# Counting 22 of 157 edge groups with matrix products instead of 24, and fetching 18 tiles of rows one row at a time from SyncE

## The chip, the core and the metric

The kernel runs on one core of a Trainium2 chip. Five engines work side by side, each through its own list of instructions in order: TensorE (PE; its weight loads are shown apart as PEld), VectorE (DVE), ScalarE (ACT), GpSimd (POOL) and SyncE (SP, which only issues transfers). They wait for each other by semaphores. The metric is the device time of one execution in microseconds (us).

## The reference

One layer of a graph network over 12500 nodes with 256 features and 200000 edges, sorted by their target `dst`. The sum over the edges is the part that this change touches.

```python
h = jnp.maximum(_layernorm(x, axis=-1), 0.0)
agg = jax.ops.segment_sum(h[src], dst, num_segments=N)
z = (1.0 + eps_gin) * h + agg
t = jnp.dot(z, W1) + b1
t = jax.nn.relu(_batchnorm(t, g1, bt1))
conv_out = jnp.dot(t, W2) + b2
out = jax.nn.relu(_batchnorm(conv_out + h, g2, bt2))
return x + out
```

## The kernel before

The edges are cut into 1563 tiles of 128 edges, and ten tiles make a group (`GT` = 10): 157 groups, the last one with three tiles. A group's edges all end in a narrow stretch of nodes, since the edges are sorted. `h_tab` in device memory holds for each node the 2 KB row of h, split into two parts that add up to full precision.

Most groups are **gathered groups**. For each of the ten tiles POOL issues one indirect transfer (`gather`, L665), which fetches 128 rows of `h_tab` by `src` into a place called `gt`; there are three such places (`RING` = 3), and the gather of a group waits until the group three before it has been read. VectorE builds ten one-hot matrices of `dst` (`edges`, L716), and TensorE multiplies the ten tiles of rows by them and adds them up in `ps` (`sums`, L748).

The other 24 groups are **counted groups**, in two sets of 12 (`SETS`, `JOINT`). They fetch no rows by index. The whole table `h_tab` is streamed past them instead, in 98 blocks of 128 nodes, through a ring of ten places (`stream`, loaded by SyncE at L963). For each counted group and each eight blocks there is one **unit**: VectorE marks which edge has its source in which of the eight blocks (`marks`, `mk`, L991), TensorE multiplies the marks by one-hots of the low seven bits of `src` (`fill`, L1008: ten products of 96 columns into `pm`), ScalarE copies the counts out of `pm` (L1012), TensorE multiplies the counts by the eight blocks (`weigh`, L1024: eight products of 512 columns), and VectorE adds the result to the group's accumulator (`collect`, L1041). A set of 12 groups takes 13 x 12 units, so there are 312 units in all. The low one-hots of a set lie in **homes**: three in a tile `away` (`AWAY` = 3), three in the still unused tile of the weights `w2s`, and twelve in `spread`.

Whichever way a group was summed, its result is then placed at its nodes: `hold` copies it (L809 to L811), `put` multiplies it by a one-hot (L834), `add` adds it into a chunk `zc` of 512 nodes (L851). A finished chunk is multiplied by W1 in four slices (`slice_of`, L861), each of which is written to `t_tab` by SyncE (L879).

The program has four stages. The lead stage (34 steps, one group each) computes h from x and sums the first 34 groups from x itself. The **middle stage** has one step for each remaining gathered group of the line except the last five. In a step the code issues one gather (four steps ahead), one sum, the placing of one or two groups, one or two slices, and as many units as `plan` has given this step: `plan` walks through the steps with two budgets (TensorE columns by a `rate`, VectorE cycles by `BUSY`), and the lowest rate is taken at which all units end in time. The works of a step are interleaved: unit, sum, placing, unit, placing or slice, and so on. A short stage then finishes the last groups, and the last stage applies the two normalisations and W2. The order of each engine's list is that of the code (`manual_schedule`).

SyncE's list in the middle stage holds the loads of `stream` (each waits until TensorE has read the block that lay there), the stores to `t_tab` (each waits for ScalarE's copy `ts`) and the loads of `zc`.

Of the kernel before, what the change touches and what calls it, by code (L numbers as in the profile page):

```python
# [9 lines left out]
F32 = mybir.dt.float32  # L10
F32R = mybir.dt.float32r
F8 = mybir.dt.float8e4
I32 = mybir.dt.int32
# [5 lines left out]
P = 128  # L19
# [5 lines left out]
LEAD = 34  # L25
# [6 lines left out]
SETS = 2  # L32
JOINT = 12
WIN = 12
# [3 lines left out]
BUSY = 12500  # L38
AWAY = 3
EASE = 3  # L40
# [9 lines left out]
def kernel(  # L50
# [328 lines left out]
    def fast():  # L379
# [24 lines left out]
        with ExitStack() as fs:  # L404
# [14 lines left out]
            with ExitStack() as es:  # L419
# [223 lines left out]

                groups = [(t0, min(GT, NTILE - t0)) for t0 in range(0, NTILE, GT)]
                gathered = {i: early[i] for i in range(EARLY)}
                landing = [tc.alloc_semaphore(f"whole{k}") for k in range(AHEAD + 1 + RING)]
# [6 lines left out]
                def gather(i):  # L653
# [7 lines left out]
                    else:  # L661
                        ga = ((0, GT, singles[k - EARLY]),)
                    for t in reversed(range(t0, t0 + n)):
                        rows = left if t == full_tiles else P
# [4 lines left out]
                        if i < NG - 2:  # L669
                            tc.no_tile_sem_insts.add(fetch.ins.name)  # L670
                            tc.add_to_no_dep_group(f"rows{i}", fetch.ins)
                            fetch.then_inc(inside if t > t0 else landing[place_of(i)], 16)
                    if i < NG - 2:
# [59 lines left out]
                def sums(i, among=()):  # L733
# [7 lines left out]
                    for k, j in enumerate(order):  # L741
# [4 lines left out]
                        if i >= LEAD:  # L746
                            lhsT, rhs, to = lhsT.bitcast(F32R), rhs.bitcast(F32R), ps.rearrange("p k d -> p (k d)")
                        reader = nc.tensor.matmul(to, lhsT=lhsT, rhs=rhs, start=(j == order[0]), stop=(j == order[-1]))  # L748
                        if waited:
                            behind(i, reader)  # L750
                            waited = False
# [341 lines left out]
                for i in range(LEAD):  # L1093
# [48 lines left out]

                    for n in range(max(JOINT * (i - LEAD + 4) // 4, 0), JOINT * (i - LEAD + 5) // 4):
                        low_digits(n)
                    sums(i, (puts, slice_ups))
# [29 lines left out]
                for s in range(LEAD, LAST):  # L1175
# [46 lines left out]
                    for k in range(1, max(len(counting), len(others) - 1)):  # L1222
                        works += counting[k : k + 1] + others[k + 1 : k + 2]
                    for work in works:
                        work()
                    while whole < NCH and all(k in done for k in touching[whole]):
                        queue += [(whole, f) for f in range(HC)]
                        whole += 1
# [605 lines left out]
```

## Time and profile before

| | |
|---|---|
| median of 3 runs | 2436.89 us (2431.2 to 2457.89) |
| the profiled execution | 2432.64 us, its span 2430.7 us |
| TensorE busy | 1808.9 us, 74% |
| VectorE busy | 1445.2 us, 59% |
| ScalarE busy | 826.6 us, 34% |
| GpSimd busy | 1332.5 us, 55% |
| mean granted TensorE clock | 0.879 |
| transfers | 513.28 MB, mean 211 GB/s |

Busy time is the union of an engine's instructions. Waiting, and the instructions that only issue transfers or set registers, do not count, so SyncE has no busy time; its transfers' issue appears as "SPq". The granted clock is the share of the full TensorE clock in that stretch. A line such as "POOL gt L665 <- PE ps L748" reads: the gather of line 665 stood idle until the sum of line 748 had finished.

### The profile page before, as it was taken

Reading aid. Unit: us, or ns where it says so; the run is one execution under the profiler, and the core shown is the slowest. Engines: PE = TensorE matmul, PEld = TensorE weight load, DVE = VectorE, ACT = ScalarE, POOL = GpSimd, SP = SyncE. Lnnn points to the kernel's source line nnn. Section 1 sums busy time; section 2 is a strip of 40 time slices with the busy share of each in tenths; the row PEclk is TensorE's granted clock in tenths of the full one; section 3 lists DMA queues with packets and bytes.
Section 4 is the critical chain, followed back from the end, with each engine's and each line's share of the span. In section 5 each row is a group of like instructions: output and inputs, shape, how many; then the busy total and the mean of one; then the engine's idle time right before and its main releaser. Section 6 shows DMA issues by size and latency. Waiting matters only on the chain. (4 is left out here: it accounts for less than half of the span.)

```text
span 2430.7 us, 25628 instructions
## 1 busy us (share of the span) xinstructions
PE 1808.9 (74%) x8988; PEld 1277.0 (53%) x8988; DVE 1445.2 (59%) x2244; ACT 826.6 (34%) x1608; POOL 1332.5 (55%) x1372
## 2 busy tenths in 40 slices
PE   1566666637787788888786788788787877658997
PEld 1444444525565566556554556566565655425445
DVE  4565666636466565565556655555555655544897
ACT  1675656613322222222221222222222222112555
POOL 7666666653565555556545565555555545442550
PEclk9876887868998999899987899999898988689999
DMA  5667677656676766666666676676776756466888
GB/s 165 206 221 237 205 244 222 196 154 198 209 217 201 209 197 209 195 213 203 214 179 190 202 239 205 194 213 201 215 212 198 220 180 219 126 172 218 307 306 335
DMA packets 195410, 513.28 MB, mean 211 GB/s; under 512 B 30358, under 2 KB 45626, under 8 KB 195272
## 3 DMA queue, kind: packets, MB, share of 16 engines
q0 software_dynamic: 94928, 302.21, 42.5%
q1 hardware_dynamic: 98960, 208.29, 25.1%
q8 instruction: 73, 1.20, 0.2%
q10 hardware_dynamic: 1384, 1.06, 0.2%
q14 instruction: 65, 0.53, 0.1%
HBM read 434.64 MB, written 76.80 MB: 210 GB/s over the span
## 5 line engine op out<-in xcount | busy, mean ns | idle before, releaser
L665 POOL DMA_INDIRECT gt<-h_tab,srcT x983 | 930.2, 946 | 786.2 <-PE ps L748 453.4
L1024 PE MATMUL pz<-stream,counts 128*120 128x512 f32 (+1 forms) x2352 | 702.3, 445 | 26.5 <-issue 14.2
L1012 ACT CAST counts<-pm 128x480 fp32r<-128x480 f32 (+1 forms) x600 | 308.2, 556 | 843.9 <-PE pm L1008 387.0
L1024 PEld LDWEIGHTS pz<-stream,counts 128*120 128x120 f32 (+1 forms) x2352 | 453.7, 204 | 136.1 <-issue 17.3
L991 DVE SCALAR_TENSOR_TENSOR mk<-col,dstT 128x960 fp8e4<-128x960 f32 (+5 forms) x328 | 340.8, 1043 | 0.0
L1041 DVE TENSOR_TENSOR gta<-pz,gta 120x512 f32<-120x512 f32 x192 | 132.3, 689 | 325.4 <-PE pz L1024 198.2
L716 DVE TENSOR_TENSOR oh<-col,dstT 128x1280 fp32r<-128x1280 f32 (+1 forms) x131 | 194.2, 1483 | 150.3 <-remote 87.0
L748 PE MATMUL ps<-gt,oh 128*128 128x512 f32 x970 | 259.7, 417 | 0.0
L861 PE MATMUL ph<-zc,w1s 128*128 128x512 f32 (+1 forms) x392 | 207.0, 657 | 49.7 <-issue 19.1
L748 PEld LDWEIGHTS ps<-gt,oh 128*128 128x128 f32 x970 | 199.8, 207 | 49.5 <-issue 1.0
L1008 PE MATMUL pm<-mk,spread 128*128 128x96 fp8e4 (+1 forms) x1560 | 100.9, 210 | 115.8 <-issue 49.8
L1008 PEld LDWEIGHTS <-spread 128*128 128x128 fp8e4 x1560 | 79.8, 101 | 170.4 <-issue 109.9
L878 ACT COPY ts<-ph 128x512 f32<-128x512 f32 x96 | 56.0, 584 | 331.5 <-issue 176.4
L1041 DVE TENSOR_TENSOR gtb<-pz,gtb 120x512 f32<-120x512 f32 x96 | 66.1, 689 | 152.5 <-PE pz L1024 94.5
L665 POOL DMA_INDIRECT stream<-in_x_dram,srcT x130 | 124.3, 956 | 57.4 <-issue 28.8
L851 DVE TENSOR_TENSOR zc<-pz,zc 128x512 f32<-128x512 f32 (+15 forms) x227 | 110.4, 513 | 72.1 <-PE pz L834 38.0
L861 PEld LDWEIGHTS ph<-zc,w1s 128*128 128x128 f32 x392 | 81.4, 214 | 124.8 <-issue 80.6
L872 DVE BATCH_NORM_STATS2 st<-ph 128x6 f32<-128x512 f32 x96 | 66.8, 696 | 132.1 <-PE ph L861 63.3
L834 PE MATMUL pz<-at,zh 128*128 128x256 f32 (+2 forms) x484 | 100.0, 318 | 56.2 <-issue 16.9
L834 PEld LDWEIGHTS pz<-at,zh 128*128 128x128 f32 (+1 forms) x484 | 79.4, 206 | 89.1 <-issue 39.7
L665 POOL DMA_INDIRECT gta<-in_x_dram,srcT x96 | 92.7, 966 | 50.4 <-issue 17.3
L1008 PE MATMUL pm<-mk,away 128*128 128x96 fp8e4 (+1 forms) x780 | 52.8, 215 | 74.2 <-DVE mk L991 33.3
(247 smaller groups left out, 2271.6 us busy)
## 6 DMA issues: line engine op xcount, KB each, us to landing
stream<-h_tab SPq DMA_DIRECT2D x201, 256.0 KB
h_tab<-gt SPq DMA_DIRECT2D x24, 1024.0 KB
t_tab<-ts SPq DMA_DIRECT2D x96, 256.0 KB
gt<-h_tab,srcT POOLq DMA_INDIRECT x983
gt<-in_x_dram SPq DMA_DIRECT2D x24, 512.0 KB
h_cols<-gt SPq DMA_DIRECT2D x24, 512.0 KB
zc<-h_cols SPq DMA_DIRECT2D x24, 512.0 KB
yT<-h_cols SPq DMA_DIRECT2D x24, 512.0 KB
```

The lines of the kernel that those rows point to most:

```text
L665: fetch = nc.gpsimd.indirect_dma_start(out=slot(ga, t - t0)[:rows], out_offset=None, in_=x if i < LEAD else h_tab, in_offset=bass.Indirect ...
L716: nc.vector.tensor_tensor(oh.bitcast(F32R) if i >= LEAD else oh, col[:, :P].unsqueeze(1).to_broadcast([P, n, P]), dstT[:, t0 : t0 + n].uns ...
L748: reader = nc.tensor.matmul(to, lhsT=lhsT, rhs=rhs, start=(j == order[0]), stop=(j == order[-1]))
L834: nc.tensor.matmul(pz[:, d, :n], lhsT=zs[:rows, k, d * P : (d + 1) * P].bitcast(F32R), rhs=at[:rows, :n].bitcast(F32R), start=(k == 0), st ...
L851: nc.vector.tensor_add(side, pz[:, :, a - lo : b - lo], side)
L861: nc.tensor.matmul(ph[:, :n], lhsT=w1s[:, d, f * P : (f + 1) * P], rhs=zc[c][:, d, :n], start=(d == 0), stop=(d == DC - 1),)
L872: nc.vector.bn_stats(st1[:, f, c, :], ph[:, :n])
L991: nc.vector.scalar_tensor_tensor(mk[:, :, done * WIN : done * WIN + w], col[:, :w].unsqueeze(1).to_broadcast([P, GT, w]), float(a0 * WIN), ...
L1008: nc.tensor.matmul(pm[:, k, :], lhsT=digits[z][j][:, t0 + k, :], rhs=marked[n][:, t0 + k, :w], start=True, stop=True,)
L1012: nc.scalar.copy(counts[n][:, :nb, :].bitcast(F32R).rearrange("p a (t d) -> p t a d", d=WIN)[:, t0 : t0 + m], pm.rearrange("p t (a d) -> p ...
L1024: nc.tensor.matmul(products[n][:ROWS], lhsT=counts[n][:rows, k, :].bitcast(F32R), rhs=ring[(b0 + k) % len(ring)][:rows].bitcast(F32R), sta ...
L1041: nc.vector.tensor_add(acc[j][:ROWS], got, acc[j][:ROWS])
```

## The change

**Two sets of 11 counted groups** (`JOINT` = 11). The line of gathered groups grows by two, from 133 to 135, and the middle stage from 94 to 96 steps. A set takes 13 x 11 units, so 286 are left of 312. The planner's lowest rate becomes 24400 (26500 before); its units end in step 126 (123 before). Of the steps, before and now, 6 and 25 have two units, 40 and 41 have three, 41 and 24 have four; three steps have another number.

**Homes.** `away` holds one home, not three, and `spread` eleven, not twelve, which makes room for two places of 128 x 512 numbers, called `apart`. The moments at which the second set's one-hots are written follow from the homes that come free, as before. Of the first set's one-hots seven are written in the three steps before the last of the lead stage and four in the last one (three in each step before).

**18 tiles row by row.** Every fifth step from step 42 to 127 the gathered group loses the first of its ten tiles: POOL issues nine indirect transfers for it. SyncE fetches that tile instead, over the five steps that end two steps before the sum: 28 rows in each of the first four, 16 in the fifth. At a step's first part SyncE reads 28 row numbers from a tile in on-chip memory into its registers (the tile `vrows`, whose 18 rows are loaded with the numbers at the start of the fast path). For each row it computes an address and issues one transfer of 2 KB. The rows are spread over the parts of the step, behind each part's own transfers. TensorE waits, ahead of the last of the ten products of that sum, for the semaphore of the tile's 128 rows.

SyncE's list around a boundary of two such steps, now (L1015 is the load of a `stream` block, L669 the reading of the row numbers, L679 the address and the row):

```order
L679 DMA apart<-h_tab 1x512
L1015 DMA stream<-h_tab 128x512
L669 TENSOR_LOAD vrows
L679 ISA
L679 DMA apart<-h_tab 1x512
L679 ISA
L679 DMA apart<-h_tab 1x512
```

The same list in the middle stage before (L963 is the load of a `stream` block, L879 the store of a slice, L705 the load of a chunk):

```order
L963 DMA stream<-h_tab 128x512 x2
L879 DMA t_tab<-ts 128x512
L963 DMA stream<-h_tab 128x512 x2
L879 DMA t_tab<-ts 128x512
L963 DMA stream<-h_tab 128x512 x3
L705 DMA zc<-h_cols 128x1024
L963 DMA stream<-h_tab 128x512 x7
```

Every load of a block and every store now has several pairs of address and row in front of it on the same queue.

ScalarE's list shows how many units a step has, since each unit has two copies of counts and each step begins with one L809. A stretch early in the middle stage, before (L1012 copies counts, L878 a slice):

```order
L809 CAST zh<-ps 128x256
L1012 CAST counts<-pm 128x5x8x12 x4
L878 COPY ts<-ph 128x512
L1012 CAST counts<-pm 128x5x8x12 x2
L809 CAST zh<-ps 128x256
L1012 CAST counts<-pm 128x5x8x12 x8
L809 CAST zh<-ps 128x256
```

And a stretch at about the same place now (the same copies, at lines 861, 1064 and 930):

```order
L861 CAST zh<-ps 128x256
L1064 CAST counts<-pm 128x5x8x12 x4
L930 COPY ts<-ph 128x512
L861 CAST zh<-ps 128x256
L1064 CAST counts<-pm 128x5x8x12 x8
L861 CAST zh<-ps 128x256
L1064 CAST counts<-pm 128x5x8x12 x8
L861 CAST zh<-ps 128x256
L1064 CAST counts<-pm 128x5x8x12 x6
```

Steps of two units with one slice have come in beside those of three and four. TensorE's list at a sum of a group that has lost a tile, before and now (the first row is a unit's `weigh`, the second the sum, then the placing):

```order
L1024 MATMUL pz_4265<-stream,counts 120x512 x8
L748 MATMUL ps<-gt,oh 128x512 x10
L834 MATMUL pz_4288<-at,zh 128x256 x4
L1008 LDWEIGHTS w2s
L1008 MATMUL pm<-mk,w2s 128x96
```

```order
L1076 MATMUL pz_6740<-stream,counts 120x512 x8
L795 MATMUL ps<-gt,oh 128x512 x9
L795 MATMUL ps<-apart,oh 128x512
L886 MATMUL pz_6829<-at,zh 128x256 x4
L1060 LDWEIGHTS away
```

Nine products read the gathered tiles, and the tenth reads the place that SyncE has filled. The diff:

```diff
-JOINT = 12
+JOINT = 11
...
-AWAY = 3
+AWAY = 1
+GAP = 5
+ASK = 28
...
                 groups = [(t0, min(GT, NTILE - t0)) for t0 in range(0, NTILE, GT)]
+                alone = {line[s]: k for k, s in enumerate(range(LEAD + 8, LAST - 1, GAP))}
+                assert len(alone) <= VN and GAP * ASK >= P
+                numbers = vrows.bitcast(I32)
+                for i, k in alone.items():
+                    first = groups[i][0] * P
+                    nc.sync.dma_start(
+                        numbers[k : k + 1, :], src[first : first + P].rearrange("(o e) -> o e", o=1)
+                    )
+                apart_sem = [tc.alloc_semaphore(f"apart{k}") for k in range(2)]
+                places_apart, at_row, asked = {}, {}, {}
+
+                def rows_apart(s, part, parts_):
+
+                    for i, k in alone.items():
+                        begin = pos[i] - GAP - 1
+                        if not begin <= s < begin + GAP:
+                            continue
+                        if i not in places_apart:
+                            places_apart[i] = wide.tile([P, 2 * D], F32, name="apart", bufs=2)
+                            at_row[i] = 0
+                        if part == 0:
+                            known = range(ASK * (s - begin), min(P, ASK * (s - begin + 1)))
+                            _, values = nc.values_load_multi_w_load_instructions(
+                                numbers[k : k + 1, known[0] : known[-1] + 1], engines=[mybir.EngineType.SP],
...
+                            )
+                            asked.update(zip(known, values))
+                        a, upto = at_row[i], min(P, ASK * (s - begin) + ASK * (part + 1) // parts_)
+                        at_row[i] = max(a, upto)
+                        for p in range(a, upto):
+                            value = asked.pop(p)
+                            row_in = nc.sync.dma_start(
+                                places_apart[i][p : p + 1, :], h_tab[bass.ds(value, 1), :]
+                            )
...
+                            row_in.then_inc(apart_sem[k % 2], 16)
...
-                    for t in reversed(range(t0, t0 + n)):
+                    t_end = t0 + (i in alone)
+                    for t in reversed(range(t_end, t0 + n)):
...
+                        lonely = j == 0 and i in alone
+                        if lonely:
+                            assert at_row[i] == P
+                            nc.tensor.wait_ge(apart_sem[alone[i] % 2], 16 * P * (alone[i] // 2 + 1))
+                            rhs = places_apart.pop(i).bitcast(F32R)
                         reader = nc.tensor.matmul(to, lhsT=lhsT, rhs=rhs, start=(j == order[0]), stop=(j == order[-1]))
...
-                    for n in range(max(JOINT * (i - LEAD + 4) // 4, 0), JOINT * (i - LEAD + 5) // 4):
-                        low_digits(n)
+                    clear = min(cut + len(homes) - after, JOINT)
+                    made = [clear * k // 3 for k in range(4)] + [JOINT]
+                    if i >= LEAD - 4:
+                        for n in range(made[i - LEAD + 4], made[i - LEAD + 5]):
+                            low_digits(n)
...
-                    for work in works:
+                    for k, work in enumerate(works):
                         work()
+                        rows_apart(s, k, len(works))
```

More of the change, by code (lines that the diff above doesn't have):

```diff
@@ L644, in fast @@
                 groups = [(t0, min(GT, NTILE - t0)) for t0 in range(0, NTILE, GT)]
+                alone = {line[s]: k for k, s in enumerate(range(LEAD + 8, LAST - 1, GAP))}
[20 more added lines that the diff above has]
+                                numbers[k : k + 1, known[0] : known[-1] + 1], engines=[mybir.EngineType.SP],
+                                min_val=0, max_val=N - 1,
+                                skip_runtime_bounds_check_because="src holds row numbers of x",
+                            )
[7 more added lines that the diff above has]
+                            )
+                            tc.no_tile_sem_insts.add(row_in.ins.name)
+                            tc.add_to_no_dep_group(f"apart{i}", row_in.ins)
+                            row_in.then_inc(apart_sem[k % 2], 16)
                 gathered = {i: early[i] for i in range(EARLY)}
@@ L671, in gather @@
                             tc.add_to_no_dep_group(f"rows{i}", fetch.ins)
-                            fetch.then_inc(inside if t > t0 else landing[place_of(i)], 16)
+                            fetch.then_inc(inside if t > t_end else landing[place_of(i)], 16)
                     if i < NG - 2:
@@ L747, in sums @@
                             lhsT, rhs, to = lhsT.bitcast(F32R), rhs.bitcast(F32R), ps.rearrange("p k d -> p (k d)")
-                        reader = nc.tensor.matmul(to, lhsT=lhsT, rhs=rhs, start=(j == order[0]), stop=(j == order[-1]))
+                        lonely = j == 0 and i in alone
[3 more added lines that the diff above has]
+                            rhs = places_apart.pop(i).bitcast(F32R)
+                        reader = nc.tensor.matmul(to, lhsT=lhsT, rhs=rhs, start=(j == order[0]), stop=(j == order[-1]))
+                        if lonely:
+                            tc.declare_no_dep(
+                                reader.ins, group=f"apart{i}", reason="its engine waits for the rows' semaphore"
+                            )
+                            tc.declare_fence(reader.ins, group=f"apart{i}")
                         if waited:
```

## The prediction

> **What bounds the kernel now.** I read the page first, then the busy times by stage; the middle stage runs from the first to the last sum at L748.
>
> ```profile
> span 2430.7 us, 25628 instructions
> PE 1808.9 (74%) x8988; PEld 1277.0 (53%) x8988; DVE 1445.2 (59%) x2244; ACT 826.6 (34%) x1608; POOL 1332.5 (55%) x1372
> ```
>
> ```profile
> core 0: us, PE busy (x) PEld busy (x) DVE busy (x) ACT busy (x) POOL busy (x), PEclk, DMA share, GB/s
> 541.60:2109.90 1568.30, 1251.03 (x7122) 914.32 (x7121) 906.79 (x1273) 409.50 (x831) 851.52 (x900) 0.90 0.67 202
> ```
>
> The middle stage is 1568.3 of 2430.7 us. TensorE is busy for 1251.0 of them (80%), no other engine above 58%; the remaining 317 us of TensorE are waits. The waits and the sums of this stage say who waits for whom:
>
> ```profile
> L748 PE MATMUL ps<-gt,oh x901: 387/393/775, 566.8 to 2109.9; 128*128 128x512 f32 x181
> POOL gt L665 <- PE ps L748: 374.4, 64, 11.2
> PE pm L1008 <- issue: 98.0, 58, 4.1
> PE pm L1008 <- DVE mk L991: 93.1, 61, 3.2
> PE pm L1008 <- ACT counts L1012: 53.2, 28, 4.1
> ```
>
> 901 products are 90 groups and the start of another, so 90 steps take 1543.1 us, 17.15 us each. GpSimd waits 374 us for TensorE to read its old rows; TensorE has no wait of weight for gathered rows. Its waits stand before the fills of units: for marks, for counts, or for nothing that the profile names. So TensorE and the chain through its units set the pace. One step with nothing in its way shows what the parts cost (start, duration; one row is one work):
>
> ```profile
> 1775.34 2.45 PE L748 MATMUL ps<-gt,oh 128*128 128x512 f32 x10
> 1777.63 0.63 PE L834 MATMUL pz<-at,zh 128*128 128x256 f32 x4
> 1778.10 0.60 PE L1008 MATMUL pm<-mk,spread 128*128 128x96 fp8e4 x10
> 1778.52 2.10 PE L1024 MATMUL pz<-stream,counts 128*120 128x512 f32 x8
> 1780.46 1.88 PE L861 MATMUL ph<-zc,w1s 128*128 128x512 f32 x4
> 1782.17 0.59 PE L1008 MATMUL pm<-mk,spread 128*128 128x96 fp8e4 x10
> ...
> 1788.58 2.45 PE L748 MATMUL ps<-gt,oh 128*128 128x512 f32 x10
> ```
>
> From start to start: a sum 2.29, a placing 0.47, a unit 2.36 (1778.10 to 1780.46), a slice 1.71 us; three units and two slices make 13.24 us. The average step has 312/90, about 3.4, units.
>
> **The change, part by part.**
>
> *26 units fewer.* The unit's lower price is the clean 2.36 us. Its mean busy price comes from the windows of the two lines in the stage (weigh L1024, then fill L1008, then the sums L748 for later):
>
> ```profile
> 580.80:2109.90 1529.10, 698.10 (x2337) 450.90 (x2336) 0.90 0.68 204
> 580.80:2109.90 1529.10, 202.33 (x3090) 159.28 (x3090) 0.90 0.68 204
> 580.80:2109.90 1529.10, 230.89 (x891) 179.19 (x891) 0.90 0.68 204
> ```
>
> 3090 fills are 309 units: (698.1 + 202.3) / 309 = 2.91 us. The upper price charges all waits and slices to units: (17.15 - 2.29 - 0.47) / 3.43 = 4.20 us. I take 2.91, the middle row: part of the waits will shrink with the units, but not all belong to them. 26 x 2.91 = -75.8 us (bounds -61.4 and -109.2). VectorE and ScalarE lose their share of the units too, beside it.
>
> *Two gathered groups more.* 20 products at 230.89/891 = 0.26 us: +5.2 us. Placing costs the same for either kind of group. Two more steps bring two more step starts; if all waits belonged to steps, that is 2 x 317/90 = 7.0 us, if none, 0; I take +3.3.
>
> *GpSimd.* It issues 20 gathers more and 18 fewer. Consecutive gathers start 1.25 us apart:
>
> ```profile
> 836.51 0.94 POOL L665 DMA_INDIRECT gt<-h_tab,srcT  x1 [0.30 <-issue]
> 837.76 0.94 POOL L665 DMA_INDIRECT gt<-h_tab,srcT  x1 [0.30 <-issue]
> ```
>
> Ten make 12.5 us a step, and its 374 us of waiting cover the two extra ones (2.5 us if that cover were gone). A step with two units and a slice, 2.29 + 0.47 + 2 x 2.91 + 1.71 = 10.3 us, is shorter than 12.5; there are 25 of them, not 6. The places hold three groups, so longer neighbours average this out. I take 0 here, +19 x 2.2 = +42 if nothing averages.
>
> *2304 rows on SyncE.* No such transfer with an address from a register stands in the trace. The nearest rows are these: two loads of one row each, a load of a block, the reading of one register, and the slowest issue of a plain load:
>
> ```profile
> L225 SPq DMA_DIRECT2D rawi_d<-in_dst_dram x2: 223/223/223, 2.4 to 7.4; - x2
> L225 SPq DMA_DIRECT2D rawi_s<-in_src_dram x2: 234/242/251, 8.2 to 8.5; - x2
> L963 SPq DMA_DIRECT2D stream<-h_tab x193: 319/320/687, 585.2 to 2065.6; - x193
> L1799 SPq TENSOR_LOAD <-flag x1: 470/470/470, 28.0 to 28.0; - x1
> L1321 SPq DMA_DIRECT2D gta<-in_x_dram x4: 737/932/953, 2288.7 to 2324.8; - x4
> ```
>
> So a row costs between 0.22 and 0.95 us of SyncE. I take 0.30: nearest to the one-row loads, plus something for the address instruction, which no row prices. 2304 x 0.30 + 90 x 0.47 = 733 us. What it lies beside is SyncE's own waiting:
>
> ```profile
> SPq L963 <- PE pz L1024: 490.5, 94, 14.4
> SPq L879 <- ACT ts L878: 150.5, 19, 29.6
> SPq L963 <- PE pm L1008: 138.0, 19, 10.4
> SPq L963 <- remote: 137.7, 21, 13.0
> ```
>
> These four give 917 us of cover. Queued behind each burst of rows are the loads of `stream`, for which TensorE waits, and the stores of slices, for which ScalarE's two `ts` buffers wait. A step's 28 rows are spread over some nine parts, so a load finds about three rows, 0.9 us, ahead of it. By the code a block is requested about four units before its use, over 9 us even at the clean price. So: 0 us. TensorE's new wait finds its last row requested a whole step earlier: 0 us.
>
> *The transfers of the rows.* They bring the bytes that POOL's 18 tiles no longer bring, but in 2304 packets:
>
> ```profile
> q1 hardware_dynamic: 98960, 208.29, 25.1%
> ```
>
> A mean packet of 2.1 KB takes 0.251 x 16 x 2430.7 / 98960 = 0.099 us. Spread over 16 engines that is nothing: 14 us each. All on one it is 228 us, beside the 0.67 x 1568 = 1051 us which that engine already has in the stage: 1279 of some 1500. [...]
>
> *The start.* The 18 loads of row numbers come ahead of SyncE's first loads of x:
>
> ```profile
> 33.09 4.19 SPq L402 DMA_DIRECT2D gt<-in_x_dram  x4
> ```
>
> SyncE had its register at 28.5 us and waited until 33.1 for the places; 18 x 0.25 = 4.5 us fit in there. 0 us, +5 without that cover. The homes and the written moments of one-hots only move: 0 us.
>
> Sum: -75.8 + 5.2 + 3.3 = -67.3 us. The profiled execution took 2432.6 us, so 2365.3; the median of the three runs lies 4.3 us above it: 2370 us.
>
> **The rivals.**
>
> *The freed time is lost to TensorE's clock (no change).* Two neighbouring stretches differ in it:
>
> ```profile
> 1300.00:1400.00 100.00, 78.05 (x387) 54.27 (x388) 64.20 (x112) 23.15 (x52) 60.19 (x64) 0.83 0.69 201
> 1400.00:1500.00 100.00, 82.41 (x466) 58.72 (x465) 57.35 (x79) 29.93 (x61) 59.34 (x63) 0.97 0.76 227
> ```
>
> The stretch with fewer units (1300 to 1400, around the change of sets) has the lower clock, 0.83 against 0.97. Steps with two units leave more gaps. If the stage's clock fell from 0.90 to 0.85, 1185 us of busy time would grow by 1185 x (0.90/0.85 - 1) = 70 us, and the gain is gone: 2440 us. Against it: the step shown above has only three units and no gap at all. The Trainium skill ("TensorE: Matmul & The Clock Gate", Part 1) has this as a rule: after a window of about 3.4 us without enough work the array's clock is halved. By that rule the time given back depends on where the gaps lie, not on their sum. No row here tells whether gaps get longer or fewer. Chance 0.20.
>
> *SyncE becomes the bound (slower).* In a fetching step it has on average 25.6 rows, one register reading, two blocks and a store. Its stage offers 1529 us; blocks and stores take about 100 us and readings 42, so rows may take (1529 - 142) / 2304 = 0.60 us before SyncE alone needs the old stage's time. From there each 0.02 us more on a row costs 46 us. At 0.63 us the stage is 69 us longer: 2506 us. For it speaks the 0.93 us row, against it the two one-row loads. Chance 0.13.
>
> *One transfer engine is full (slower).* If a packet of a row takes 0.25 us, not 0.099, that engine needs 1051 + 576 = 1627 us in a stage of 1568, and landings set the pace: +59 us, 2496 us. The low share of 0.67 before speaks against it. Chance 0.05. That the change does not do what it says is excluded by the order of the instructions above.
>
> **How the numbers follow.** Forecast 0.62: 2370 us. Its own range: from -109.2 + 5.2 (2333) to -61.4 + 5.2 + 7.0 + 2.5 + 5 (2395). Runs of this kernel tell about 1% (24 us) from no change. Faster by over 1%: 0.62; within it: the clock rival, 0.20; slower: 0.13 + 0.05. The range 2333 to 2445 takes in the forecast and the clock rival and leaves out the two slow ones.
>
> **What would show it.** Right: 286 units in the middle stage, a mean step near 16 us, GpSimd still waiting for sums, a row on SyncE at 0.25 to 0.4 us, no wait of TensorE at the tenth product of a shortened sum. Wrong: the block loads issued late and TensorE waiting for `stream`; SyncE with no waits left; a granted clock near 0.85; a row above 0.5 us.

## The result, and the profile after

The changed kernel takes 2769.07 us in the median, the kernel before 2440.75 us beside it. The ratio is 1.1311, with a 95% interval from 1.124 to 1.1382. It is slower by 13%, where 2370 us had been predicted. One of its five executions took 5387.49 us; it counts in the median and not in the ratio. The profiled execution took 2773.39 us.

The page of the kernel after shows the busy times of its engines and the chain that ended last, first by engine and then by line:

```profile
span 2771.6 us, 31654 instructions
PE 1830.9 (66%) x8552; PEld 1278.6 (46%) x8552; DVE 1405.8 (51%) x2192; ACT 804.4 (29%) x1556; POOL 1338.0 (48%) x1374
...
PE 29%; issue 22%; SPq 21%; DVE 11%; another core or an unknown queue 9%; ACT 4%; DMA 4%; ACTq 0%; DVEq 0%
SPq L679 16%; PE pz L1076 11%; PE ps L795 5%; PE ph L913 3%; PE pm L1060 3%; DMA stream<-h_tab 2%; SPq L669 2%; DVE stg L558 2%; PE one L1429 2%; DVE oh L758 1%; PE pr L1429 1%; PE pq L1429 1%; SPq L1015 1%; PE pz L886 1%
```

The 436 products fewer on TensorE are there (8988 before), and yet its busy time did not fall (1808.9 us before): the stretch from 600 to 1700 us had a granted clock of 0.91 before and has 0.80 now. No engine is busy for more than 66%.

```profile
core 0: us, PE busy (x) PEld busy (x) DVE busy (x) ACT busy (x) POOL busy (x), PEclk, DMA share, GB/s
600.00:1700.00 1100.00, 720.44 (x3732) 520.10 (x3732) 492.87 (x700) 220.12 (x443) 494.97 (x522) 0.80 0.56 168
```

The longest single line of the chain is L679, the one-row transfers of SyncE. These are the instructions of that line, of the readings of row numbers (L669) and of the block loads (L1015), each as count, then shortest, median and longest duration in ns, then first and last start:

```profile
L679 SPq FUSED_REGOPS  x2304: 1/37/1325, 604.1 to 2464.6; - x192
L679 SPq MOVE apart<-h_tab x2304: 2/29/1397, 604.2 to 2464.6; - x192
L679 SPq DMA_DIRECT2D apart<-h_tab x2304: 2/228/1397, 604.2 to 2464.7; - x192
L669 SPq TENSOR_LOAD <-vrows x90: 3/1836/2865, 601.1 to 2456.8; - x90
L1015 SPq DMA_DIRECT2D stream<-h_tab x203: 2/362/702, 567.6 to 2456.4; - x102
```

A row is three instructions, not one. In the median, neighbouring rows start 0.412 us apart, in the mean 0.672 us (worked out from the start times of the 2058 pairs with nothing else between them). So SyncE spends 2304 x 0.672 = 1548 us on rows, up to 90 x 1.84 = 165 us on readings and 82 us on the 270 other transfers among them: some 1795 of the 1860 us between the first and the last row. It is full, and its waits of before are gone. Of 490.5 us of waiting for TensorE to read a block 5.3 us are left, and of the waiting for the copies `ts` only 2.4 us fall between the first and the last row (the line below counts the whole execution):

```profile
SPq L931 <- ACT ts L930: 168.4, 17, 74.9
SPq L1015 <- PE pz L1076: 5.3, 11, 2.5
```

In their place stands a wait that TensorE did not have: for blocks that were requested late. GpSimd, in turn, waits 817.6 us for TensorE's sums in the whole execution, where it waited 453.4 us. (The last line is from the page before: the gathers, their busy time and mean, then the idle time ahead of them and how much of it ended with a sum.)

```profile
PE pz L1076 <- DMA stream<-h_tab: 190.4, 39, 15.2
PE pm L1060 <- issue: 171.8, 66, 6.5
PE pm L1060 <- ACT counts L1064: 110.0, 29, 19.6
POOL gt L707 <- PE ps L795: 817.6, 82, 47.4
```

```profile
L665 POOL DMA_INDIRECT gt<-h_tab,srcT x983 | 930.2, 946 | 786.2 <-PE ps L748 453.4
```

One such case, as the timeline has it (start, duration, what; several neighbours of one kind stand in one row). First SyncE, then GpSimd's gathers of the same time, the first and the last of ten, then TensorE:

```profile
1006.99 1.05 SPq L679 DMA_DIRECT2D apart<-h_tab  x3
1008.14 0.36 SPq L1015 DMA_DIRECT2D stream<-h_tab  x1
1009.90 14.54 SPq L679 DMA_DIRECT2D apart<-h_tab  x16
1024.45 0.35 SPq L931 DMA_DIRECT2D t_tab<-ts  x1
1024.90 0.87 SPq L1015 DMA_DIRECT2D stream<-h_tab  x2
```

```profile
1010.27 0.95 POOL L707 DMA_INDIRECT gt<-h_tab,srcT  x1 [13.66 <-PE ps L795]
...
1021.55 0.95 POOL L707 DMA_INDIRECT gt<-h_tab,srcT  x1 [0.31 <-issue]
```

```profile
1027.99 0.78 PE L1076 MATMUL pz<-stream,counts 128*120 128x512 f32 x1 [12.54 <-DMA stream<-h_tab]
...
1034.58 2.22 PE L795 MATMUL ps<-gt,oh 128*128 128x512 f32 x9
1036.64 0.40 PE L795 MATMUL ps<-apart,oh 128*128 128x512 f32 x1
```

Sixteen rows, 0.9 us each, hold SyncE from 1009.90 to 1024.45 while the ten gathers are issued; three rows ahead of the gathers take 1.05 us together. The two block loads behind the sixteen are issued at 1024.90, and TensorE, which needed the first, has stood for 12.54 us when it starts at 1027.99. The tenth product of the shortened sum, on the other hand, follows the nine others at once: the rows themselves are there in time. In 15 of the 18 shortened sums it starts 0.23 us after the ninth, and at most 1.15 us after it.

### The profile page after: what moved, and what is told of

It is laid out like the page before. It is cut to its first block, busy times and chain, and to the rows that moved or that the text cites. A ratio compares the mean times of both kernels' runs of the same rounds, so it can differ in the third digit from the quotient of the medians.

```text
span 2771.6 us, 31654 instructions
## 1 busy us (share of the span) xinstructions
PE 1830.9 (66%) x8552; PEld 1278.6 (46%) x8552; DVE 1405.8 (51%) x2192; ACT 804.4 (29%) x1556; POOL 1338.0 (48%) x1374
## 3 DMA queue, kind: packets, MB, share of 16 engines
q1 hardware_dynamic: 103604, 213.03, 22.7%
q8 instruction: 70, 1.15, 0.2%
## 4 chain that ended last, share of the span: by engine, by line
PE 29%; issue 22%; SPq 21%; DVE 11%; another core or an unknown queue 9%; ACT 4%; DMA 4%; ACTq 0%; DVEq 0%
SPq L679 16%; PE pz L1076 11%; PE ps L795 5%; PE ph L913 3%; PE pm L1060 3%; DMA stream<-h_tab 2%; SPq L669 2%; DVE stg L558 2%; PE one L1429 2%; DVE oh L758 1%; PE pr L1429 1%; PE pq L1429 1%; SPq L1015 1%; PE pz L886 1%
## 5 line engine op out<-in xcount | busy, mean ns | idle before, releaser
L707 POOL DMA_INDIRECT gt<-h_tab,srcT x985 | 934.0, 948 | 1127.7 <-PE ps L795 817.6
L1076 PE MATMUL pz<-stream,counts 128*120 128x512 f32 x2156 | 705.5, 473 | 237.7 <-DMA stream<-h_tab 190.4
L1076 PEld LDWEIGHTS pz<-stream,counts 128*120 128x120 f32 x2156 | 448.0, 220 | 368.6 <-DMA stream<-h_tab 211.4
L1064 ACT CAST counts<-pm 128x480 fp32r<-128x480 f32 (+1 forms) x550 | 285.3, 556 | 1089.6 <-PE pm L1060 527.1
L1043 DVE SCALAR_TENSOR_TENSOR mk<-col,dstT 128x960 fp8e4<-128x960 f32 (+4 forms) x300 | 312.0, 1045 | 0.0
L1060 PE MATMUL pm<-mk,spread 128*128 128x96 fp8e4 (+1 forms) x1820 | 131.8, 224 | 226.7 <-issue 102.3
L913 PE MATMUL ph<-zc,w1s 128*128 128x512 f32 (+1 forms) x392 | 219.1, 690 | 75.6 <-issue 39.8
L795 PE MATMUL ps<-gt,oh 128*128 128x512 f32 x972 | 266.0, 424 | 0.0
L1060 PEld LDWEIGHTS <-spread 128*128 128x128 fp8e4 x1820 | 104.2, 109 | 292.9 <-issue 246.2
L1093 DVE TENSOR_TENSOR gtb<-pz,gtb 120x512 f32<-120x512 f32 x72 | 49.6, 689 | 193.6 <-PE pz L1076 99.6
L1060 PE MATMUL pm<-mk,w2s 128*128 128x96 fp8e4 (+1 forms) x780 | 55.6, 221 | 92.3 <-issue 60.2
```

What stands on the lines that cost most here:

```text
L707: fetch = nc.gpsimd.indirect_dma_start(out=slot(ga, t - t0)[:rows], out_offset=None, in_=x if i < LEAD else h_tab, in_offset=bass.Indirect ...
L913: nc.tensor.matmul(ph[:, :n], lhsT=w1s[:, d, f * P : (f + 1) * P], rhs=zc[c][:, d, :n], start=(d == 0), stop=(d == DC - 1),)
L1043: nc.vector.scalar_tensor_tensor(mk[:, :, done * WIN : done * WIN + w], col[:, :w].unsqueeze(1).to_broadcast([P, GT, w]), float(a0 * WIN), ...
L1060: nc.tensor.matmul(pm[:, k, :], lhsT=digits[z][j][:, t0 + k, :], rhs=marked[n][:, t0 + k, :w], start=True, stop=True,)
L1064: nc.scalar.copy(counts[n][:, :nb, :].bitcast(F32R).rearrange("p a (t d) -> p t a d", d=WIN)[:, t0 : t0 + m], pm.rearrange("p t (a d) -> p ...
L1076: nc.tensor.matmul(products[n][:ROWS], lhsT=counts[n][:rows, k, :].bitcast(F32R), rhs=ring[(b0 + k) % len(ring)][:rows].bitcast(F32R), sta ...
```

## The experiments

The theory after this reading: SyncE's own list is the bound (readings, address instructions and issues add up), and blocks come late behind it. Its rivals: the transfers or their number disturb the rest; the units that went were worth nothing; TensorE's clock.

The kernel before took about 1920 us in four series of these runs and 2437 or 2552 us in two, and its time within a series varied by about 1% to either side (one execution of 2028 us apart). Ratios are therefore taken within a series, and each series is named by the time of the kernel before in it. (Two series that bear the same chip's number gave 2437 and 1923 us, so it is not shown that this belongs to a chip.) The profile before, on which the prediction rests, is of the slower kind; no profile of the kernel before was taken in the other.

The kernels with fixed rows, with one reading, with the counter and with one piece leave out the row numbers of `src`. They fetch other rows, so they show what the work costs and do not compute the layer.

### First series: the parts taken apart (the kernel before: 1924.82 us)

The expectations of this series were priced for a kernel before of 2440 us, so their times in us cannot be met here; only the ratios tell.

No rows: `alone` is empty, GpSimd fetches all tiles; the sets of 11 stay.

```
-alone = {line[s]: k for k, s in enumerate(range(LEAD + 8, LAST - 1, GAP))}
+alone = {}
```

> Two sets of 11 counted groups, the homes and the plan of the changed kernel, but POOL fetches all ten tiles of every group: no rows on SyncE. Theory A (SyncE's rows are the whole loss): the time falls under the kernel before, to about 2370 us as the prediction's sum had it, with SyncE waiting for TensorE again. Rival B (the plan, the homes or the two extra gathers are at fault): it stays above 2450 us.

Measured: 1934.86 us, ratio 1.0053 (1.0032 to 1.0073). The 26 units that went brought nothing here, so neither of the two expectations holds.

Rows alone: sets of 12 as before, 17 tiles row by row.

```
-JOINT = 11
-AWAY = 1
+JOINT = 12
+AWAY = 0
...
-spare_digits = wide.tile([P, AWAY * GT * P // 4], F32, name="away")
+spare_digits = None
```

> Two sets of 12 as before, 312 units, but 17 tiles are fetched row by row (for the room, away has no home at all). Theory A: 2176 rows at the 0.67 us that the changed kernel shows, and 85 readings of row numbers, need about 1590 us of SyncE in 87 steps that took 1490 us: about 2700 to 2800 us, SyncE without waits. Rival B: within 30 us of the kernel before.

Measured: 2056.3 us in one run, 6.8% above the kernel before.

Half of the tiles: nine, over ten steps each.

```
-GAP = 5
-ASK = 28
+GAP = 10
+ASK = 14
...
-range(LEAD + 8, LAST - 1, GAP)
+range(LEAD + 12, LAST - 1, GAP)
```

> The changed kernel with 9 tiles instead of 18 fetched by rows, 14 rows a step over ten steps: the rate on SyncE is halved. Theory A: 12.8 rows a step at 0.67 us and a reading of 1.5 us are some 10 us of a 16 us step, so SyncE keeps waits and the time is within 30 us of the kernel without rows. If rows also hurt below the saturation of SyncE (by the loads behind them or by the one transfer engine), the time lies halfway, near 2570 us. Rival B: as the changed kernel, 2770 us.

Measured: 1933.04 us in one run, 0.4% above. Half of the rows cost next to nothing where all of them cost 7 to 9%.

Fixed rows: the row numbers stand in the program, so that readings and address instructions are gone and 2304 transfers stay.

```
-_, values = nc.values_load_multi_w_load_instructions(...)
-asked.update(zip(known, values))
+asked.update((p, 97 * p + 3 * k) for p in known)
...
-    places_apart[i][p : p + 1, :], h_tab[bass.ds(value, 1), :]
+    places_apart[i][p : p + 1, :], h_tab[value : value + 1, :]
```

> The changed kernel with fixed row numbers: no reading of row numbers and no address instruction, the same 2304 transfers of 2 KB (the rows are not those of src). If the cost of a row is SyncE's own instructions, a row falls from 0.41 to about 0.27 us without a gather beside it, the waits beside gathers shrink as well, and the time falls by 300 us or more. If a row waits for its turn behind gathers on a transfer engine, it keeps about 0.9 us beside a gather, and the time stays above 2600 us.

Measured: 1912.45 us in one run, 0.6% below the kernel before. The transfers, their bytes and their number are not the loss in this series; what goes with the row numbers is.

### Second series: the change again (the kernel before: 2437.41 us)

> The changed kernel itself once more, beside the kernel before, because the kernel before took 1925 us on the chip of the first experiments and 2441 us on the chip of the result. Theory A1 (SyncE's own issue is the loss wherever it runs): 2304 rows at the 0.42 us between starts that the runs of the first experiments show and 90 readings at 1.85 us are 1130 us of SyncE, so block loads come late in the fetching steps: 3 to 7% slower than before on any chip. Theory A2 (on the chip of the result a second thing stretches SyncE's work, rows at 0.9 us beside gathers): on a chip where the kernel before takes about 1925 us the rows stay at 0.42 us and the change costs under 7%; where it takes about 2440 us, rows reach 0.9 us beside gathers again and it costs about 13%.

Measured: 2767.72 us, 1.1367 (1.1281 to 1.1453). It repeats the result.

Sets of 12 with half of the tiles (the edits of the rows alone and of half of the tiles together; nine tiles, 1152 rows):

> Two sets of 12 with 312 units as before, and 8 tiles by rows at half the rate (14 rows a step over ten steps). Theory A: SyncE has room for it, so nothing is lost: within 1% of before. If GpSimd's gathers set the pace of the middle stage on that chip, 8 gathers fewer at 1.25 us give back up to 10 us (0.5% faster); on a chip where GpSimd waits for sums they give nothing. Rival: rows cost time at any rate: 2% slower or more.

Measured: 2633.01 us, 1.083 (1.0753 to 1.0907). This is a miss for the theory as it stood. Its row pitch, from the start of one row to the start of the next, is 0.45 us apart from gathers and 0.92 us beside them, 0.719 us in the mean; rows, readings (180 us) and the other transfers make 1152 x 0.719 + 180 + 89 = 1097 us, 64% of a stage of 1706 us. SyncE had waits left, and TensorE none of weight for blocks:

```profile
SPq L1015 <- PE pz L1076: 206.9, 77, 8.7
```

```profile
PE pm L1060 <- issue: 132.3, 61, 5.5
PE pm L1060 <- ACT counts L1064: 124.5, 36, 7.6
PE pm L1060 <- DVE mk L1043: 102.4, 43, 8.9
```

So in this series rows whose numbers come out of registers, with the homes that moved to make room for them, cost 196 us before SyncE is full; the two were not tried apart. The waits that grew stand ahead of the fills of the units: for counts (53.2 us in the profile before) and with no cause named (98.0 us). The wait for marks did not grow (101.9 us in the whole execution before).

### Third series: the change, no rows, fixed rows (the kernel before: 1919.72 us)

> The changed kernel once more, as the bridge between chips. Where the kernel before takes about 2440 us: 2760 us again, rows at 0.9 us beside gathers. Where it takes about 1925 us: rows at 0.42 us throughout (theory A2) and 3 to 7% slower, by 1130 us of SyncE's issue squeezed into a stage of some 1250 us; if theory A1 alone held, the same percentage would have shown on both chips.

> Two sets of 11 and no rows, again. On a chip where the kernel before takes 1925 us: the same as before within 1%, as measured. Where it takes 2440 us: theory A (rows are the whole loss) says about 2370 us, the prediction's sum, since TensorE and not GpSimd sets the pace there; rival B (fewer units and more gathers do not pay there either) says 2430 us or more.

> 2304 transfers of fixed rows, without readings of row numbers and without address instructions (the rows are not those of src). Where the kernel before takes 2440 us: if the transfers stretch the rows beside gathers, a row still takes 0.7 us or more there and the time stays above 2600 us; if the instructions around them do, it falls to 2450 us or less. Where it takes 1925 us: 1912 us again.

Measured: the change 2099.42 us, 1.0924 (1.0892 to 1.0955); no rows 1932.99 us, 1.0069 (1.0045 to 1.0092); fixed rows 1916.6 us, 0.9972 (0.9955 to 0.999). The change had been expected 3 to 7% slower here, and 9% was measured. The kernel with no rows says why fewer units don't help in such a series. This is a stretch of its middle stage, and GpSimd's gathers in the whole kernel:

```profile
core 0: us, PE busy (x) PEld busy (x) DVE busy (x) ACT busy (x) POOL busy (x), PEclk, DMA share, GB/s
600.00:1500.00 900.00, 824.30 (x5091) 611.54 (x5090) 663.85 (x934) 282.49 (x580) 674.06 (x712) 0.97 0.86 275
```

```profile
L707 POOL DMA_INDIRECT gt<-h_tab,srcT x1003 | 951.2, 948 | 323.7 <-issue 290.2 <-PE ps L795 20.1 <-PE pz L1076 6.7
```

GpSimd waits 20.1 us for sums (453.4 us in the profile of the kernel before). 712 starts in 900 us are 1.26 us each, the 1.25 us at which gathers follow each other with nothing between. GpSimd is the pace of this kernel, and the two gathered groups more give it 20 gathers, 25 us by this pace; 10 and 13 us were measured.

### Fourth series: the same three steps where it is slow (the kernel before: 2551.96 us)

The kernel with one reading: 28 numbers are read once and serve all rows; address instructions and transfers stay.

```
+if not kept_values:
     _, values = nc.values_load_multi_w_load_instructions(...)
-asked.update(zip(known, values))
+    kept_values.extend(values)
+asked.update(zip(known, kept_values))
```

> The change with one edit: the 28 row numbers are read into SyncE's registers once, and the 18 tiles take their rows from these same registers again and again. 89 of the 90 readings go; the two address instructions ahead of every row and the 2304 one-row transfers stay. The rows fetched are not the ones that src names, so the sums of these tiles are of other rows. Theory A (SyncE is the bound, and its load is the sum of readings, address instructions and issues): 89 readings of about 1.85 us are 165 us less on SyncE. Where the kernel before takes about 1920 us, the change took 2099, and this kernel should come out at 1935 to 2000. Where the kernel before takes about 2440 us, the change took 2768 with a row pitch of 0.67 us, and this kernel should come out at 2600 to 2680, still slower than before by 7% or more, since the rows alone are over 1500 us there. Theory B (rows at addresses out of registers disturb the gathers, however they are read): within 1% of the change, 2080 to 2120 or 2740 to 2790.

> The change without its row by row fetches: two sets of 11 counted groups, two fewer homes, GpSimd fetches all tiles. This is the units term of the prediction by itself: 26 units of counting fewer at 2.91 us, two more gathered groups, GpSimd with 18 tiles more than in the change. Theory A (TensorE's stream of units sets the pace): -67 us, so 0.97 of the kernel before; on a chip where that takes 2440 us it is 2365 to 2400. Theory B (GpSimd's gathers set the pace as soon as units go): 1.00 to 1.01 of the kernel before, as it was (1.005 and 1.007) where the kernel before takes 1920 us.

> The change with the row numbers written into the program: no readings, no address instructions, but the same 2304 one-row transfers on SyncE at the same places of the program. The rows fetched are not the ones that src names, so the sums of these tiles are of other rows. Theory A (SyncE's own instructions are the whole loss): 0.99 to 1.00 of the kernel before, as where it takes 1920 us (0.997 and 0.994). Theory B, for a chip where the kernel before takes 2440 us (a row that is issued beside a gather waits for it there, whatever its address comes from): 2304 rows at about 0.6 us and more are still 1400 us on SyncE, 2550 to 2680, 1.05 to 1.10 of the kernel before.

Measured: no rows 2446.15 us, 0.9577 (0.951 to 0.9645); fixed rows 2554.4 us, 1.0007 (0.9967 to 1.0046); one reading 2707.24 us, 1.0631 (1.055 to 1.0712). Here the 26 units are worth 106 us net, and the rows take that back and more, in steps: fixed rows 108 us, their addresses out of registers another 153 us. The change itself did not run in this series. The granted clock does not explain the gain or its absence: 0.854 with no rows, 0.839 to 0.857 in runs of the kernel before.

The timelines of SyncE show what registers do. With fixed rows, sixteen in 5.83 us (0.36 us each), one of the slowest groups of its window:

```profile
1033.83 4.70 SPq L674 DMA_DIRECT2D apart<-h_tab  x16
1049.34 5.83 SPq L674 DMA_DIRECT2D apart<-h_tab  x16
```

With one reading, twelve rows ahead of the gathers in 4.75 us (0.40 each), and 23 beside them in 17.25 us (0.75 each); the gathers began at 1016.33:

```profile
1010.94 4.75 SPq L681 DMA_DIRECT2D apart<-h_tab  x12
...
1018.51 17.25 SPq L681 DMA_DIRECT2D apart<-h_tab  x23
```

```profile
1016.33 0.94 POOL L709 DMA_INDIRECT gt<-h_tab,srcT  x1 [11.60 <-PE ps L797]
```

Over the whole stage the mean pitch is 0.33 us with fixed rows and 0.711 us with one reading. With fixed rows SyncE has 2304 x 0.33 + 90 = 850 us of work in a stage of 1629 us and still waits for TensorE; with one reading it has 2304 x 0.711 + 91 = 1729 of 1790 us and no longer waits:

```profile
SPq L1010 <- PE pz L1071: 151.4, 59, 8.8
SPq L1010 <- PE pm L1055: 124.2, 22, 9.9
```

```profile
SPq L1017 <- PE pz L1078: 9.6, 20, 2.0
```

So with one reading SyncE's list fills the stage, and the 108 us of fixed rows were lost while it still had time. That the 153 us are the full list alone is not shown. TensorE's waits for late blocks are 42.0 us, while the waits ahead of the fills with no cause named grew from 143.6 us with fixed rows to 321.5 us:

```profile
PE pm L1055 <- issue: 143.6, 66, 6.4
```

```profile
PE pm L1062 <- issue: 321.5, 98, 12.0
PE pz L1078 <- DMA stream<-h_tab: 42.0, 8, 12.8
```

The profiles of the slower series lack many records of semaphores (see the end), so the names of waits in them are less sure than in the others.

### Fifth and sixth series: register instructions, and one transfer for a tile (1924.13 and 1923.33 us)

The counter kernel: fixed rows, and ahead of each a register instruction whose result no address uses, but for the very last row's. The one-piece kernel: each of the 18 tiles by one transfer of 128 adjacent rows. Both edits are shown against the kernel with fixed rows.

```
+nc.sync.reg_alu(counter, counter, 1, OP.bitwise_xor)
...
 row_in = nc.sync.dma_start(places_apart[i][p : p + 1, :], h_tab[value : value + 1, :])
```

```
-for p in range(a, upto):
-    row_in = nc.sync.dma_start(places_apart[i][p : p + 1, :], h_tab[value : value + 1, :])
+if a < P <= upto:
+    row_in = nc.sync.dma_start(places_apart[i], h_tab[k * P : (k + 1) * P, :])
...
-nc.tensor.wait_ge(apart_sem[alone[i] % 2], 16 * P * (alone[i] // 2 + 1))
+nc.tensor.wait_ge(apart_sem[alone[i] % 2], 16 * (alone[i] // 2 + 1))
```

> The change itself, beside the two kernels that follow it, so that their differences can be taken on one chip. Where the kernel before takes 1920 us, 1.09 of it; where it takes 2440 us or more, 1.12 to 1.14 of it.

> The change with fixed rows (no readings, no address instructions; the rows fetched are not the ones that src names), and ahead of each of the 2304 one-row transfers one register instruction on SyncE that flips a bit of a register which no row's address uses. It asks what the address instructions cost where the kernel before takes 2440 us or more: fixed rows alone gave 1.0007 of the kernel before there, rows from registers without the readings 1.063. Theory A (any register instruction between the transfers is held beside the gathers, because SyncE's next instruction comes late): the row pitch is 0.6 us and more in the mean, and the time 1.03 to 1.07 of the kernel before. Theory B (only a transfer whose address comes from registers is held): the pitch is 0.3 to 0.4 us and the time 0.995 to 1.015. Where the kernel before takes 1920 us both expect 0.99 to 1.01, since nothing was held there.

> The change with each of the 18 tiles fetched by one transfer of 128 adjacent rows on SyncE, in place of 128 transfers of one row; the same bytes, places, waits and the same 18 gathers fewer on GpSimd, and the rows are not the ones that src names. It asks what the number of transfers costs by itself, since fixed rows cost 106 us more than no rows where the kernel before takes 2550 us, with SyncE still waiting for over 500 us. Theory A (each issue on SyncE, or each small transfer, slows the whole core there): 0.95 to 0.965 of the kernel before, as without rows. Theory B (the two places apart and the waits for them, or the bytes, slow it): 0.99 to 1.005. Where the kernel before takes 1920 us: 0.98 to 1.00 by both, since GpSimd gives up 18 gathers of 0.95 us and its pace bounds that chip.

> The kernel of c6_one_reading again: one reading of 28 row numbers, address instructions and 2304 one-row transfers kept (other rows than those of src). Where the kernel before takes 1920 us it has not run: the change is 1.09 of before there, fixed rows with a register instruction each 0.995. Theory A (SyncE's load is the sum, readings of 1.87 us among it, row pitch 0.42 us): 89 readings less are 166 us less on SyncE, 0.995 to 1.02 of before. Theory B (the address instructions and transfers out of registers are the loss): 1.05 to 1.09. Where before takes 2440 us or more: 1.05 to 1.07, as it was.

> The kernel of f1_counter again: fixed rows (other rows than those of src) and one register instruction on SyncE ahead of each transfer, which no address uses. Where the kernel before takes 2440 us or more: theory A (any register instruction between the transfers is held beside the gathers) a mean row pitch of 0.55 us or more and 1.03 to 1.07 of before; theory B (only a transfer addressed from registers is held) 0.3 to 0.4 us and 0.995 to 1.015. Where before takes 1920 us: 0.995, as it was.

> The kernel of f2_one_piece again: each of the 18 tiles by one transfer of 128 adjacent rows (other rows than those of src). Where the kernel before takes 2440 us or more: theory A (the number of transfers costs by itself) 0.95 to 0.965 of before; theory B (places, waits or bytes) 0.99 to 1.005. Where before takes 1920 us: 0.998, as it was.

Measured: the change 2093.93 us, 1.089 (1.0851 to 1.093); the counter 0.9947 (0.9923 to 0.9971) and 0.996 (0.9947 to 0.9973); one piece 0.9979 (0.9962 to 0.9996) and 0.9953 (0.9932 to 0.9973); one reading 1949.1 us, 1.0132 (1.011 to 1.0154). Both series were of the kind in which the kernel before takes 1920 us, so the two questions for the other kind stay open. In this kind they settle the readings: from the change to one reading are 1.089 - 1.0132 = 0.076, about 146 us, for readings that take 163 us together. From one reading to the counter kernel, which has a cheaper register instruction in place of the two, are 31.5 us. In the change of this kind a row's three instructions stay near their shortest durations, and no row is held beside a gather (the longest issue takes 431 ns):

```profile
L679 SPq FUSED_REGOPS  x2304: 37/37/51, 505.8 to 1785.1; - x192
L679 SPq MOVE apart<-h_tab x2304: 29/29/38, 505.9 to 1785.2; - x192
L679 SPq DMA_DIRECT2D apart<-h_tab x2304: 224/228/431, 506.0 to 1785.3; - x192
```

And yet SyncE is full: 2304 x 0.421 + 163 + 99 = 1232 us of 1279 us, and blocks come late as in the result:

```profile
PE pz L1076 <- DMA stream<-h_tab: 125.6, 43, 9.5
```

SyncE's load in the stage of the rows against the time, for the kernels of this kind (pitch worked out from the start times as above):

| kernel | SyncE's list, us | of the stage, us | share | time against before |
|---|---|---|---|---|
| half of the tiles | 1152 x 0.424 + 184 + 99 = 771 | 1098 | 70% | 1.004 |
| fixed rows | 2304 x 0.306 + 93 = 798 | 1089 | 73% | 0.997 |
| one reading | 2304 x 0.422 + 100 = 1072 | 1131 | 95% | 1.013 |
| rows alone, sets of 12 | 2176 x 0.421 + 152 + 96 = 1164 | 1203 | 97% | 1.068 |
| the change | 2304 x 0.421 + 163 + 99 = 1232 | 1279 | 96% | 1.089 |

Up to three quarters of the stage the list costs nothing. With fixed rows the stage takes 1089 us; a list of 1072 us, just under that, costs 1.3%, and with longer ones the stage is 3 to 4% longer than the list. From one reading to the change, both with 18 tiles, the list grows by 160 us and the time by 145.

## Why the prediction was wrong

**The step that failed** is "2304 rows on SyncE", with its "So: 0 us". What was laid into the cover (917 us of waits on SyncE) was 733 us by the prediction's prices for rows and readings. Measured, SyncE's list with the rows takes some 1795 us, of which up to 1713 us are rows and readings. Nor is such cover free where the kernel before takes 2440 us or more: in the fourth series fixed rows cost 108 us while SyncE still waited. Three sizes were off:

- A row's instructions. I took 0.30 us, from the duration of the one-row loads plus something. The transfer's own 0.228 us was near the row quoted, but address instruction, move and the gaps between make 0.412 us where nothing holds them.
- What holds them. Beside gathers the rows of the result stand 0.9 us apart, so the mean is 0.672 us. No row of the trace before showed that.
- A reading. I took 0.47 us from a reading of one number; 28 numbers take 1.84 us in the median, 16 of them 1.17 us. In the kernel with half of the tiles readings of 14 numbers take 1.37 or 3.08 us in turn (the longer ones start at number 14, 42, 70 or 98 of the tile) and those of two numbers 0.67 us. I had priced the instruction, not what it reads; but the durations don't go with the count alone, and what sets them was not tried.

The argument that "a load finds about three rows, 0.9 us, ahead of it" also failed by an average. Not every part of a step has a load or a store of its own: the 2304 rows stand in 246 stretches with no other work of SyncE between, 9.4 rows in the mean, and 16 or 23 in 29 of them. Sixteen rows at 0.9 us are 14.5 us ahead of a block, more than the "over 9 us" by which a block is requested early.

**The rival that came true** is "SyncE becomes the bound", given 0.13. Its mechanism and its place are those of the trace: SyncE without waits, late blocks, TensorE waiting for `stream`. Its break-even of 0.60 us a row rested on the cheap reading; with 1.84 us it is (1529 - 100 - 165) / 2304 = 0.55 us. At 0.672 us its own arithmetic gives (0.672 - 0.55) x 2304 = 281 us over the time before, 2722 us; 2769 was measured. The last 47 us stay unexplained, as do the 108 us of fixed rows in the fourth series and the 196 us of half of the tiles in the second: there time is lost with rows on SyncE while SyncE still has time, and no run here shows by what.

The Trainium skill ("DMA: Bandwidth & Descriptors", "Issuing engines are not separate DMA queues") says that the sequencer's time to initiate a transfer is usually small beside the transfer. For the block loads the traces agree: 0.36 us of issue for 256 KB, against 3.1 us from issue to the waiting product in the case shown (1024.90 to 1027.99). For rows they don't: a row takes 0.412 us of SyncE, and a mean packet of that queue 0.227 x 16 x 2771.6 / 103604 = 0.097 us. The 2304 issues fill SyncE, while the transfer engines are busy for only 0.56 of the stretch from 600 to 1700 us.

```profile
q1 hardware_dynamic: 103604, 213.03, 22.7%
```

**The units** were right in kind and too small in size where the kernel before takes 2440 us or more, as in the prediction's profile: the kernel without rows gains 106 us in the fourth series (of 2552 us), where -67 us was the sum. That is (106 + 8.5) / 26 = 4.4 us a unit, just above the upper price of 4.20, and the middle row of 2.91 was too low a choice there. Where the kernel before takes 1920 us the gain is none: in the kernel without rows GpSimd has hardly any waiting left. The prediction named that cover (374 us in the middle stage). Its price for the loss of it, "2.5 us if that cover were gone", is for the change, in which SyncE takes 18 of the 20 new gathers off GpSimd. The kernel without rows has all 20, and it is 10 to 13 us slower.

**The rest.** The transfers at 0 us are borne out in their place: the tenth product follows the ninth, by 1.15 us at most. The page counts 4644 packets more on that queue than before (98960), which is two for each of the 2304 rows and 18 loads of numbers; on which engines they ran it does not show. The start at 0 us is borne out by the kernels with fixed rows, which keep its 18 loads and lose nothing where the kernel before takes 1920 us. The clock rival fell: with fewer units and no rows the clock was as before and the gain came (fourth series). The clock of 0.80 in the stage after goes with TensorE's new waits; whether it adds to them was not tried.

No version was faster than the kernel before in both kinds of series. The sets of 11 without rows gain 4.2% in the series of 2552 us and lose 0.5 and 0.7% in two of 1920 us.

## What to carry to other kernels

Before work is laid on an engine that only issues transfers, write its list as instructions: every address instruction, every register reading by what it reads, every issue, from start to start and not by duration. Compare the sum with the shortest stage that you hope for, and look at the longest burst ahead of a transfer that somebody needs, not at the mean one. An engine's waits are cover only up to the point where they are used up; from there nearly each microsecond on its list was one of the kernel's here (145 of 160). And in the slower series time was lost before that point, so leave a margin.

## What was not expected of the hardware

- The same kernel took 1920 us in some series and 2437 to 2552 us in others. The instructions last the same in both (a gather 948 ns and 945 ns in the kernel without rows, third and fourth series); in the slower series they start later, often with no cause that the profile names, and the records of semaphores are fewer than the instructions that signal (977 of 1605 on VectorE in the fourth series, all of them in the third). Whether the missing records and the late starts have one cause was not tried.
- In the slower series SyncE's instructions of register-addressed rows are held beside GpSimd's gathers. In the kernel with one reading the starts of neighbouring rows that are held stand mostly near 0.7, 1.4 and 2.1 us apart (292 of 2073 pairs between 1.4 and 1.5, 110 between 2.1 and 2.2, none between 1.5 and 1.9). With fixed addresses the longest is 1.5 us, with 14 such pairs. In the series of 1920 us no two neighbouring rows of the change start more than 0.78 us apart. Whether it is the register instructions or the transfers addressed by registers that are held is open: the counter kernel, made for that question, ran only where nothing is held.
- Reading 28 numbers from on-chip memory into SyncE's registers takes 1.84 us, and SyncE does nothing else meanwhile. Taking 89 of the 90 readings away gave back about 146 us where SyncE is full.
